# Moving small vector steps to GpSimd and ScalarE, routing ahead of other steps, and a constant product in rounds without a step: attention with a sparse expert layer, one core

## The chip, the cores and the metric

The kernel runs on 1 core of one Trainium2 chip. The time is device microseconds (us) of that core for one execution, from three runs, of which the median is given. A separate execution was profiled; its trace gives the durations of single instructions. Engines are written as in the profile: PE is TensorE's matmul, PEld its weight load, DVE is VectorE, ACT is ScalarE, POOL is GpSimd, SP is SyncE.

## The reference

Input x has shape (8, 512, 128): 8 sequences (B) of T = 512 rows with D = 128. All is float32.

```python
q, k1, k2, v = heads(x @ Wq.T), heads(x @ Wk1.T), heads(x @ Wk2.T), heads(x @ Wv.T)   # 16 heads of 8
a1 = softmax(causal(q @ k1 / sqrt(8)));  a2 = softmax(causal(q @ k2 / sqrt(8)))
attn = a1 - sigmoid(lambda)[head] * a2
attn = attn / max(sum(abs(attn)), 1e-6)
x = layernorm(x + (attn @ v) @ Wo.T)
xn = layernorm(x) * gamma + beta                     # the expert layer, 8 experts, 2 per row
probs = softmax(xn @ router_w.T / 1.5);  w, idx = top_k(probs, 2)
y = sum over the 2 experts of w * (silu(xn @ W1[e]) @ W2[e])        # W1: 128x512, W2: 512x128
out = layernorm(x + y)
```

## The kernel before, in words

**Attention by units.** A unit (class `Unit`) is one sequence b and one group j of 32 queries for all 16 heads; its keys reach L = 32(j+1). Four heads share the 128 partitions, so a unit has four groups g of four heads. There are 8 x 16 = 128 units. Up to L = 256 a unit is called early and has 2 slots of scores (both softmaxes of two groups in one tile); above that it has 4 slots (two groups, one softmax). This makes 8 x (8 x 2 + 8 x 4) = 384 rounds, one per slot.

**What a slot goes through.** `scores` (PE, L327 and the causal mask L336, tile `sc`, two buffers), `maxima` (DVE, L349 and L357, negated row maxima `nm`), `exps` (ACT, L367, tile `et`, with the row sums in `sums`). After a unit's last slot, `combine` runs by pieces (two groups at a time for early units, one group for others): `ratios` (L379, L382, L383: three small DVE instructions that make c2, the ratio of the two softmax sums times lambda, once a unit), then per group a DVE scalar_tensor_tensor (L393, tile `junk`, only its row sum is kept: it gives the sum of absolute values), then per group a POOL multiplication of the second softmax by -c2 in place (L403), and where L isn't a multiple of 128 a POOL copy `rest` (L417). Then `transposes` (PE, L448, one tile `pt` with one buffer, first and second softmax accumulated in PSUM), `evacuate` (ACT, L473, tile `aT`) and `times_v` (PE, L490, tile `po`).

**A round** (`round_of`, L1107) issues one stage of each on the engines' in-order queues, which are written out by hand here: `times_v` of the unit that is through, `scores` of the slot ahead, `evacuate`, the list `on_act`, `maxima` of the present slot, `transposes`, the list `on_dve`, `combine` of the piece or pieces that are due, `exps` of the present slot, the list `on_dve_late`. Then it hands out other steps, which put PE work at the round's end and push what reads its result on one of the lists, for the next round.

**The other steps.** Five steps for each block of 128 rows (`block_tasks`: normalise, project out and residual, norms, turn, logits) and five for the next sequence's projections (`projection_tasks`: x turned, q, k1, k2, v) share one deque, `misc`, one step a round. When a chunk of blocks (6, 9, 9, 6 and 2 blocks) is complete, `route_tasks` go through `routing`, one a round beside `misc`: top-2 choice, counts by PE, places of the rows. Then `moves` send the rows to their places in memory by indirect DMA on POOL (L777), one a round. `experts` are the steps of `sparse_tasks` for tiles of 128 rows: `turn` (PE turns the rows, L871, tile `pa`; DVE scales them by gamma and beta, L874, tile `xgT`; the second matmul of an earlier tile goes in the same PSUM tile, L880, and ACT copies it out and stores it, L890) and `hidden` (first matmul L900, tile `pz`; tanh on ACT L845; product on DVE L847, tile `hT`). The last chunk of two blocks takes `dense_tasks`. A step takes one unit of `room`, of which a round has 2; `due` and `pace` spread the experts' steps, with arrival times that `times` estimates. `gathers` fetch the results by indirect DMA on POOL (L925), mix them (L935), normalise and store (L826).

**PSUM.** Eight banks: `ps_s` two tiles `sc` of two banks, `ps_t` one, `ps_o` one, `ps_m` two tiles `pm` for all the other steps, `pa` and `pz` among them.

**After the attention** some 40 rounds without a slot take two experts' steps each; this tail holds most of the last sparse chunk (19 tiles) and the dense chunk.

Of the kernel before, what the change touches and what calls it, by code (L numbers as in the profile page):

```python
# [20 lines left out]
def kernel(  # L21
# [43 lines left out]
    nhalf = const.tile([P, CB], F32, name="nhalf")  # L65
    rank = const.tile([P, CB, E], F32, name="rank")
# [45 lines left out]
    with ExitStack() as actx:  # L112
# [123 lines left out]
        def projection_tasks(b):  # L236
# [10 lines left out]
            def transpose_x():  # L247
                pm = ps_m.tile([P, NT, P], F32, tag="pm", name=f"pmx_{b}")
                for c in range(NT):
                    nc.tensor.transpose(pm[:, c, :], xts[b][:, c, :], ident)  # L250
                on_dve.append(lambda: nc.vector.tensor_copy(xT, pm))

            def project_q():
# [13 lines left out]
                def spread():  # L267
                    nc.vector.tensor_copy(qs, pm)
                    on_pool.extend(lambda h=h: spread_head(h) for h in range(4))

                on_dve.append(spread)
# [6 lines left out]
            def project_v():  # L278
# [4 lines left out]
                def keep():  # L283
                    nc.vector.tensor_copy(vt, pm)
# [5 lines left out]
                on_dve.append(keep)  # L290
# [3 lines left out]
        class Unit:  # L294
# [80 lines left out]
            def ratios(self):  # L375

                sums, jj = self.blk["sums"], self.jj
                c1 = sp.tile([P, NG], F32, tag="c1", name=f"c1_{self.b}_{self.j}")
                nc.vector.tensor_mul(c1, sums[:, 0, jj, :], slam)  # L379
# [3 lines left out]
                nc.vector.tensor_mul(self.c2, c1, r2)  # L383

            def combine(self, piece):
# [5 lines left out]
                L = self.L  # L391
                for g in piece:
                    nc.vector.scalar_tensor_tensor(  # L393
                        junk[:, :L],
                        self.et[:, g, 1, :L],
                        self.c2[:, g : g + 1],
                        self.et[:, g, 0, :L],
                        ALU.mult,
                        ALU.max,
                        accum_out=self.blk["big"][:, self.jj, g : g + 1],  # L400
                    )
                for g in piece:
# [7 lines left out]
                    )  # L410
                for gs, lo, kw in self.blocks(piece):
# [86 lines left out]
        def block_tasks(b, i, blk):  # L498
# [88 lines left out]
            def turn():  # L587
# [4 lines left out]
                else:  # L592
                    s["xnT"] = ch.xnT[:, ci, :]
                on_dve.append(
                    lambda: nc.vector.tensor_scalar(s["xnT"], pm, gam, bet, ALU.mult, ALU.add)
# [9 lines left out]
        def route_tasks(ch):  # L605
# [57 lines left out]
            def weights():  # L663
                def step():
# [6 lines left out]
                    if ch.sparse:  # L671
# [5 lines left out]
                        ch.w = [r["rc"], cp.tile([P, CB], F32, tag="w2nd", name=f"w2nd_{n0}")[:, :nb]]  # L677
                        ch.w[0] = cp.tile([P, CB], F32, tag="w1st", name=f"w1st_{n0}")[:, :nb]
# [61 lines left out]
            def rows():  # L740
                def step():
# [9 lines left out]
                    ch.row = cp.tile([P, 2, CB], U32, tag="row", name=f"row_{n0}")  # L751
# [43 lines left out]
            def together(*steps):  # L795
                def both():
                    for step in steps:
                        step()

                return both  # L800

            if not ch.sparse:
                return [largest, first, second, weights, go]
            tasks = [largest, first, second, together(weights, chosen), counts]
            tasks += [together(starts, rows), owners]
# [44 lines left out]
        def sparse_tasks(ch):  # L850
# [15 lines left out]
            def turn(t):  # L866
# [3 lines left out]
                if t < nt:  # L870
                    nc.tensor.transpose(pm[:, 0, :], xg[t], ident)  # L871
                    xgT[t] = gp_.tile([P, P], F32, tag="xgT", name=f"xgT_{n0}_{t}")
                    on_dve.append(
                        lambda: nc.vector.tensor_scalar(  # L874
                            xgT[t], pm[:, 0, :], gam, bet, ALU.mult, ALU.add
# [21 lines left out]
            def hidden(t):  # L897
                pz = ps_m.tile([P, NF, P], F32, tag="pm", name=f"pz_{n0}_{t}")
# [146 lines left out]
        misc, routing, experts, moves, gathers = (deque() for _ in range(5))  # L1045
# [18 lines left out]
        def times():  # L1064
# [8 lines left out]
            for ch in chunks:  # L1073

                behind = seq * (24 + (2 * ch.nb + 3 if ch.sparse else 0)) / 48
# [7 lines left out]
        def round_of(now=None, ahead=None):  # L1083
# [19 lines left out]
            run(on_dve)  # L1103
            left = now["left"] if now else 2
            for _ in range(-(-len(to_combine) // left)):
                v, piece = to_combine.popleft()
                v.combine(piece)  # L1107
                to_transpose.append((v, piece))
            if now:
# [5 lines left out]
            if misc:  # L1115
                misc.popleft()()
                room -= 1
            if routing:
                step = routing.popleft()
                step()  # L1120
                room -= step.__name__ == "counts"

# [18 lines left out]
            due = min(due, 4.0)  # L1141

        with tc.manual_schedule(
# [10 lines left out]
            run(on_dve)  # L1154
# [126 lines left out]
```

## Time and profile before

| | before |
|---|---|
| median of 3 runs | 1220.2 us (1216.8 to 1223.7) |
| the profiled execution | 1212.0 us, its span 1210.1 us |
| mean granted TensorE clock | 0.927 of full speed |
| first and last maxima of the attention | 19.0 us and 1084.9 us of the span |
| DVE busy, ACT busy, POOL busy | 927.1, 780.4, 526.8 us |
| DVE instructions that change: L379, L382, L383 | 175, 170, 178 ns, 128 of each |
| L874 `xgT`, L595 `xnT`, copies L251, L268, L284 | 407, 402, about 690 ns; 88, 32 and 24 of them |

A group of instructions is given as its line, engine, operation, output and inputs with partitions x elements, how many there are (x), then the busy time in us and the mean ns of one, and after a second bar how long the engine had been idle just before them and what ended that. A stretch ("windows") gives each engine's busy time in us with its number of instructions, the granted PE clock as a share of full speed, and the share of the DMA engines in use. A wait gives the engine and line that waited, what ended the wait, the total in us, how often, and the longest. A matmul of float32 is two instructions in the trace.

### The profile page before, as it was taken

The numbers are of one execution on the slowest core, as the hardware profiler recorded it, in microseconds if no ns is written. First come the engines' busy times: TensorE is split into PE (matmuls) and PEld (weight loads), VectorE is DVE, ScalarE is ACT, GpSimd is POOL, SyncE is SP. The second block draws the span as 40 slices with busy tenths as digits, with TensorE's granted clock in tenths as the row PEclk, the third lists the DMA queues.
The fourth block names the chain that finished last, engine by engine and source line by source line (L and its number), as shares of the span: only waits on it lengthen the run. The fifth ranks groups of instructions, "written<-read, shape, count | busy, mean of one in ns | idle before, by whom it ended". The sixth has DMA issues, their size and how long they took to land.

```text
span 1210.1 us, 28192 instructions
## 1 busy us (share of the span) xinstructions
PE 1093.9 (90%) x9450; PEld 776.2 (64%) x9450; DVE 927.1 (77%) x2837; ACT 780.4 (64%) x2775; POOL 526.8 (44%) x935
## 2 busy tenths in 40 slices
PE   5999899989999899989998999988999989997686
PEld 3566565555666566666666666666667667777675
DVE  4688778777887887987887878887767898874556
ACT  3678767576777777766766867774567566662221
POOL 4343433463423442267464432333554652444333
PEclk7699969797999999989998999997899799998998
DMA  4400000110221112100322222221213344444762
GB/s 133 122 8 1 10 2 8 31 56 30 50 63 46 54 32 67 45 27 27 93 69 58 73 54 68 64 73 31 81 52 91 95 120 124 122 123 129 207 177 67
DMA packets 128895, 84.28 MB, mean 70 GB/s; under 512 B 22896, under 2 KB 114288, under 8 KB 128752
## 3 DMA queue, kind: packets, MB, share of 16 engines
q1 hardware_dynamic: 111952, 68.26, 20.2%
q0 software_dynamic: 3840, 7.87, 2.3%
q10 hardware_dynamic: 12960, 6.36, 1.8%
q8 instruction: 75, 1.23, 0.4%
q14 instruction: 68, 0.56, 0.2%
HBM read 63.31 MB, written 17.56 MB: 67 GB/s over the span
## 4 chain that ended last, share of the span: by engine, by line
PE 60%; DVE 16%; ACT 11%; issue 6%; POOL 4%; DMA 3%; ACTq 1%; POOLq 0%; SPq 0%; DVEq 0%
PE pt L448 19%; PE sc L327 13%; ACT et L367 7%; PE po L490 5%; PE pz L900 5%; PE pa L880 5%; PE sc_None L327 5%; DVE junk L393 2%; DVE nm L357 2%; PE pmo L541 2%; ACT aT L473 2%; DVE nm L349 2%; POOL et L403 1%; DVE hT L847 1%; POOL xs L777 1%
## 5 line engine op out<-in xcount | busy, mean ns | idle before, releaser
L403 POOL TENSOR_SCALAR et<-et,c 128x224 f32<-128x224 f32 (+15 forms) x512 | 270.9, 534 | 458.1 <-DVE junk L393 295.0
L448 PE MATMUL pt<-ident,et 128*128 128x128 f32 (+1 forms) x2048 | 326.7, 296 | 26.8 <-ACT aT L473 14.9
L448 PEld LDWEIGHTS pt<-ident,et 128*128 128x128 f32 (+1 forms) x2048 | 230.5, 145 | 159.6 <-issue 58.2
L367 ACT ACTIVATE et<-sc,nm 128x512 f32<-128x512 f32 (+7 forms) x512 | 300.4, 595 | 48.7 <-DVE nm L357 27.6
L357 DVE TENSOR_REDUCE nm<-sc 128x2 f32<-128x576 f32 (+7 forms) x256 | 252.0, 984 | 45.1 <-PE sc L336 44.6
L473 ACT COPY aT<-pt 128x384 f32<-128x384 f32 (+5 forms) x488 | 186.1, 407 | 134.5 <-PE pt L448 130.7
L393 DVE SCALAR_TENSOR_TENSOR junk<-et,c 128x224 f32<-128x224 f32 (+15 forms) x512 | 258.6, 505 | 9.6
L327 PE MATMUL sc<-kT,qb 32*128 32x384 f32 (+7 forms) x1024 | 246.8, 559 | 10.9 <-ACT et L367 9.6
L367 ACT ACTIVATE et<-sc_None,nm 128x256 f32<-128x256 f32 (+7 forms) x512 | 188.6, 387 | 32.0 <-DVE nm L349 22.0
L327 PE MATMUL sc_None<-kT,qb 32*128 32x512 f32 (+7 forms) x512 | 116.5, 535 | 21.8 <-ACT et L367 21.0
L900 PE MATMUL pz<-xgT,w 128*128 128x128 f32 x704 | 102.1, 291 | 18.8 <-DVE xgT L874 18.5
L349 DVE TENSOR_REDUCE nm<-sc_None 128x4 f32<-128x256 f32 (+7 forms) x128 | 96.1, 751 | 29.6 <-PE sc_None L336 29.3
L327 PEld LDWEIGHTS sc<-kT,qb 32*128 32x128 f32 x1024 | 78.3, 187 | 61.3 <-ACT et L367 27.4
L367 ACT ACTIVATION_READ_ACCUMULATOR et<-sc_None,nm 128x1 f32 x512 | 108.1, 211 | 0.0
L900 PEld LDWEIGHTS pz<-xgT,w 128*128 128x128 f32 x704 | 92.5, 204 | 23.6 <-DVE xgT L874 21.2
L367 ACT ACTIVATION_READ_ACCUMULATOR et<-sc,nm 128x1 f32 x512 | 103.9, 203 | 0.0
L880 PE MATMUL pa<-w,hT 128*128 128x128 f32 x704 | 98.1, 285 | 0.6 <-ACT ysb L890 0.6
L845 ACT ACTIVATE th<-pz 128x512 f32<-128x512 f32 x88 | 52.7, 599 | 68.9 <-PE pz L900 47.9
L880 PEld LDWEIGHTS pa<-w,hT 128*128 128x128 f32 x704 | 90.9, 202 | 1.3 <-ACT ysb L890 0.7
L777 POOL DMA_INDIRECT xs<-xh,row x60 | 65.9, 1099 | 46.9 <-DMA xs<-xh,row 31.3
L490 PE MATMUL po<-aT,vt 128*32 128x128 f32 (+1 forms) x2048 | 85.3, 290 | 0.0
L847 DVE SCALAR_TENSOR_TENSOR hT<-th,pz 128x512 f32<-128x512 f32 x88 | 60.2, 684 | 30.8 <-ACT th L845 30.6
(150 smaller groups left out, 1281.0 us busy)
## 6 DMA issues: line engine op xcount, KB each, us to landing
w<-in_w_dram SPq DMA_DIRECT2D x192, 256.0 KB
xg<-xs SPq DMA_DIRECT2D x88, 64.0 KB
ys<-ysb ACTq DMA_DIRECT2D x88, 64.0 KB
xs<-zero SPq DMA_DIRECT2D x2, 1600.0 KB
xs<-zero SPq DMA_DIRECT2D x2, 1216.0 KB
xt<-in_x_dram SPq DMA_DIRECT2D x8, 256.0 KB
out_dram<-ot SPq DMA_DIRECT2D x32, 64.0 KB
vr<-vt SPq DMA_DIRECT2D x32, 32.0 KB
```

What stands on the lines that cost most here:

```text
L327: nc.tensor.matmul(parts[gi][:, :, :L], lhsT=qb[r, j].rearrange("p h q -> p (h q)"), rhs=kT[r, sets, :L], start=True, stop=False,)
L349: nc.vector.tensor_reduce(self.nm[:, g, :], sc.rearrange("p g (s l) -> p g s l", s=2)[:, :, :, : self.L], AX.X, ALU.max, negate=True,)
L357: nc.vector.tensor_reduce(self.nm[:, g, s], sc[:, :, : self.L], AX.X, ALU.max, negate=True)
L367: nc.scalar.activation(self.et[:, g, si, : self.L], sc[:, gi, lo : lo + self.L], AF.Exp, bias=self.nm[:, g, si : si + 1], accum_out=self.b ...
L393: nc.vector.scalar_tensor_tensor(junk[:, :L], self.et[:, g, 1, :L], self.c2[:, g : g + 1], self.et[:, g, 0, :L], ALU.mult, ALU.max, accum_ ...
L403: nc.gpsimd.tensor_scalar(self.et[:, g, 1, :L], self.et[:, g, 1, :L], self.c2[:, g : g + 1], -1.0, ALU.mult, ALU.mult,)
L448: nc.tensor.matmul(pt[: len(gs) * kw, x_, :], lhsT=lhsT, rhs=ident, is_transpose=True, start=(k == 0), stop=(k == 1),)
L473: nc.scalar.copy(self.aT[: rows[done], self.used + done : self.used + end, :], pt[: rows[done], done:end, :],)
L490: nc.tensor.matmul(self.blk["po"][32 * g : 32 * g + 32, self.jj, :], lhsT=v[:rows, kb, 32 * g : 32 * g + 32], rhs=self.aT[:rows, self.at[g ...
L777: nc.gpsimd.indirect_dma_start(ch.xs[:, :], bass.IndirectOffsetOnAxis(ap=ch.row[:, k, c : c + 1], axis=0), ch.xh[:, c, :], None,)
L880: nc.tensor.matmul(pm[:, 1, :], lhsT=hT[y][:, f, :], rhs=w[y][1][:, f, :], start=(f == 0), stop=(f == NF - 1),)
L900: nc.tensor.matmul(pz[:, f, :], lhsT=w[t][0][:, f * P : (f + 1) * P], rhs=xgT[t], start=True, stop=True,)
```

## The change

- The projections' copies out of PSUM (`xT`, `qs`, `vt`), and the scaling by gamma and beta of the turned rows (`xnT` of a block, `xgT` of an expert's tile), go from DVE to ACT; the latter as an activation (Identity) with a scale and a bias per partition. The DMAs on SP that follow `vt` stay.
- `ratios`: a new step `weighted`, issued at the end of the round of a unit's last slot, makes c1 on POOL; for units above L = 256 also c2, by a power of -1 and a product on POOL. Early units keep the reciprocal and one product on DVE.
- `combine` for L <= 96: POOL's multiplication comes first, and the sum of absolute values is taken late in the round from the product, for two groups by one scalar_tensor_tensor and one reduction.
- In a round `on_dve` runs after `combine`, not before it.
- Routing goes first: in a round with a routing step no step of `misc` is taken. Projections have their own deque, after `misc`. Two pairs of routing steps are taken apart, so a sparse chunk's routing is 10 steps and not 8.
- `keep_busy`: in a round of the attention in which no step took room, PE multiplies a bf16 tile of ones (128x128) by 512 columns of ones into a tile `pm` that nobody reads.
- After the attention the experts' first matmul writes to `ps_s` tiles. Row places and weights of a chunk have 3 buffers instead of 2; one number in `times` goes from 24 to 22.

```diff
-                on_dve.append(lambda: nc.vector.tensor_copy(xT, pm))
+                on_act.append(lambda: nc.scalar.copy(xT, pm))
...
-                    nc.vector.tensor_copy(qs, pm)
+                    nc.scalar.copy(qs, pm)
...
-                    nc.vector.tensor_copy(vt, pm)
+                    nc.scalar.copy(vt, pm)
...
-                nc.vector.tensor_mul(c1, sums[:, 0, jj, :], slam)
+                if self.c2 is not None:
+                    return
...
-                nc.vector.tensor_mul(self.c2, c1, r2)
+                nc.vector.tensor_mul(self.c2, self.c1, r2)
+
+            def weighted(self):
+                self.c1 = sp.tile([P, NG], F32, tag="c1", name=f"c1_{self.b}_{self.j}")
+                nc.gpsimd.tensor_tensor(self.c1, self.blk["sums"][:, 0, self.jj, :], slam, ALU.mult)
+                if not self.early:
+                    self.c2 = sp.tile([P, NG], F32, tag="c2", name=f"c2_{self.b}_{self.j}")
+                    nc.gpsimd.tensor_tensor(
+                        self.c2, self.blk["sums"][:, 1, self.jj, :], mone, ALU.pow
+                    )
+                    nc.gpsimd.tensor_tensor(self.c2, self.c1, self.c2, ALU.mult)
...
+                    if small:
+                        both = junk[:, : m * L].rearrange("p (g l) -> p g l", g=m)
+                        nc.vector.scalar_tensor_tensor(both, second, -1.0, first, ALU.mult, ALU.max)
+                        nc.vector.tensor_reduce(big[:, g0 : g0 + m], both, AX.X, ALU.add)
+                        return
...
+                if small:
+                    on_dve_late.append(largest)
...
-                    lambda: nc.vector.tensor_scalar(s["xnT"], pm, gam, bet, ALU.mult, ALU.add)
+                    lambda: nc.scalar.activation(
+                        s["xnT"], pm, AF.Identity, bias=bet, scale=gam
+                    )
...
-            tasks = [largest, first, second, together(weights, chosen), counts]
-            tasks += [together(starts, rows), owners]
+            tasks = [largest, first, second, weights, chosen, counts]
+            tasks += [starts, rows, owners]
...
-                        lambda: nc.vector.tensor_scalar(
-                            xgT[t], pm[:, 0, :], gam, bet, ALU.mult, ALU.add
+                        lambda: nc.scalar.activation(
+                            xgT[t], pm[:, 0, :], AF.Identity, bias=bet, scale=gam
...
-                pz = ps_m.tile([P, NF, P], F32, tag="pm", name=f"pz_{n0}_{t}")
+                pool, tag = (ps_s, "sc") if attention_done else (ps_m, "pm")
+                pz = pool.tile([P, NF, P], F32, tag=tag, name=f"pz_{n0}_{t}")
...
+        def keep_busy():
+            pm = ps_m.tile([P, T], F32, tag="pm", name="pmw")
+            nc.tensor.matmul(
+                pm, lhsT=ones, rhs=ones.unsqueeze(1).to_broadcast([P, 4, P]), start=True, stop=True
+            )
...
-            run(on_dve)
             left = now["left"] if now else 2
             for _ in range(-(-len(to_combine) // left)):
                 v, piece = to_combine.popleft()
                 v.combine(piece)
                 to_transpose.append((v, piece))
+            run(on_dve)
...
-            if misc:
-                misc.popleft()()
-                room -= 1
             if routing:
                 step = routing.popleft()
                 step()
                 room -= step.__name__ == "counts"
+            elif misc or proj:
+                (misc or proj).popleft()()
+                room -= 1
+            if now and now["left"] == 1:
+                now["u"].weighted()
...
+            if now and room == 2:
+                keep_busy()
```

## The prediction

> **What bounds the kernel now.** I read the page first: shares, the row of granted clocks, the chain that ended last.
>
> ```profile
> span 1210.1 us, 28192 instructions
> ...
> PE 1093.9 (90%) x9450; PEld 776.2 (64%) x9450; DVE 927.1 (77%) x2837; ACT 780.4 (64%) x2775; POOL 526.8 (44%) x935
> ...
> PEclk7699969797999999989998999997899799998998
> ...
> PE 60%; DVE 16%; ACT 11%; issue 6%; POOL 4%; DMA 3%; ACTq 1%; POOLq 0%; SPq 0%; DVEq 0%
> ```
>
> PE carries 60% of the chain; DVE, which the change relieves, 16%. The clock falls below full speed in some twenty of forty slices. Next, stretches of the trace, in pairs at the same place of a sequence (by the maxima, one a round): units 4 to 7 cold (151) and warm (410), unit 13 cold (221) and warm (353), rounds without another step (85), a warm sequence's early units (386), the tail's sparse part (1089).
>
> ```profile
> 151.20:173.10 21.90, 21.90 (x118) 12.85 (x116) 14.33 (x53) 13.26 (x57) 7.87 (x18) 0.57 0.00 1
> 410.20:427.10 16.90, 14.87 (x129) 9.88 (x130) 14.82 (x55) 14.04 (x59) 7.97 (x18) 1.00 0.15 40
> 221.10:241.10 20.00, 19.92 (x105) 12.41 (x105) 11.99 (x34) 10.12 (x31) 11.25 (x14) 0.57 0.15 46
> 353.30:367.40 14.10, 13.70 (x121) 9.66 (x119) 12.21 (x36) 10.46 (x31) 4.76 (x8) 1.00 0.19 52
> 85.50:105.60 20.10, 19.98 (x187) 12.17 (x190) 17.27 (x43) 17.54 (x57) 6.76 (x12) 1.00 0.01 1
> 386.40:429.90 43.50, 37.63 (x377) 26.85 (x379) 35.20 (x135) 33.69 (x154) 19.42 (x41) 1.00 0.18 53
> 1089.00:1166.00 77.00, 55.15 (x439) 50.24 (x440) 42.23 (x134) 20.21 (x47) 27.78 (x33) 0.91 0.60 168
> ```
>
> Order: length, then PE, PEld, DVE, ACT, POOL, clock, DMA. The cold stretches take 21.9 for 16.9 us and 20.0 for 14.1, with fewer matmuls: 23% and 30% of cold time is lost. In long rounds (85) PE is full by its modelled ends, with ACT (17.5 of 20.1) and DVE (17.3) close behind: three engines in balance. In early units (386) PE has 5.9 us free of 43.5, DVE 8.3.
>
> **DVE relief.** Removed, by these rows and the same list's 402 ns for L595 and about 690 for the three copies:
>
> ```profile
> L874 DVE TENSOR_SCALAR xgT<-pa,gam,bet 128x128 f32<-128x128 f32 x88 | 35.8, 407 | 56.7 <-ACT ysb L890 45.8 <-PE pa L871 6.6 <-issue 2.8
> L383 DVE TENSOR_TENSOR c<-c,r 128x4 f32<-128x4 f32 x128 | 22.7, 178 | 7.0 <-DVE r L382 0.9
> L379 DVE TENSOR_TENSOR c<-sums,slam 128x4 f32<-128x4 f32 x128 | 22.4, 175 | 2.4 <-ACT et L367 2.4
> L563 POOL TENSOR_TENSOR l_rs<-l_ve,nhalf 128x2 f32<-128x2 f32 x32 | 23.2, 725 | 47.3 <-DVE c L379 33.5 <-DVE l_ve L559 13.7
> L90 POOL TENSOR_TENSOR l_rs<-l_ve,nhalf 128x1 f32<-128x1 f32 x32 | 19.0, 593 | 30.8 <-DVE l_ve L88 28.4 <-DVE c L379 2.1
> ```
>
> 64 x (175 + 170 + 178) = 33.5; 64 x 175 = 11.2; 24 x 0.69 = 16.5; 32 x 0.402 = 12.9; 88 x 0.407 = 35.8: 110 us. Besides, DVE stands 45.8 us before `xgT` until ACT has copied the same PSUM tile. In long rounds none of it counts, as PE is full. In early units about 11 (c1) + 6 (half of `xnT`) + 9 (a third of the tiles before the tail) + 13 (a third of 40 us of that standing) = 39 us leave DVE; PE's free time there, 5.9 x 8 = 47, allows it. I take 14, a third, since a round's DVE work is often covered by ACT or PE: ends 0 and 39. For L <= 96 two groups' sums cost much the same either way (at L = 64 two times 285 + 83 ns before; after, one instruction of 128 elements at 354 and a reduction at 286): 0, ends -2 and +2.
>
> **ACT load.** 24 copies of 512 at 0.59 (ACT's `kT` row) are 14 us. `xnT` and `xgT`: ACT's plain 128x128 copy is 268 ns, its exponential of 128x128 with one bias operand 369; a second operand makes 0.46, and 120 of them 55 us. They go ahead of `exps` on ACT, and behind `exps` wait the next scores, which share two PSUM tiles. PE's weight loads wait for `exps` on 109 occasions in 384 rounds (28%). Of about 119 such additions outside the tail, 28% at 0.47 are 15; two thirds lie in rounds where the same step gives PE about 1 us: +5, ends 0 and +55 (all on the path).
>
> **Ratios on POOL.** No row shows a POOL power over four columns. 593 ns for one and 725 for two give 0.99 for four; two products near POOL's shortest multiplication (128x32, 294 ns) make 1.6 us from the last exponential to c2, against DVE's 0.52. Here a rule speaks against the change: the Trainium skill (GPSIMD Engine Reference, Engine selection) wants elementwise work on VectorE, GpSimd being about twice slower with two inputs. By the rule c2 would be about 0.5 us later; by the row 1.1. The row decides. On POOL the `moves`, `gathers` and the next multiplication queue behind this wait for `exps`; on DVE `junk` and what follows. But today `junk` starts 1.5 us after a long unit's last exponential (median of 64; quartiles 0.8 and 2.2), behind `on_dve` and the ratios, which now go behind or away. With each unit's own slack of the transposes behind it (median 0.8 us), a c2 1.7 us late adds 10 us of PE standing and earlier starts give 9 back. About a third of the rounds also carry an indirect DMA on POOL, so some 20 of 64 units find it occupied: +5, ends -9 and +25.
>
> **The constant product.** Counting the steps that the planner's deques hand out round by round, 111 of 384 rounds take none now, and 113 after: 113 products. No row shows a bf16 product of 512 columns; a float32 pass of 512 (L275) takes about 0.5 us in a pair, so 0.2 to 0.5. I take 0.25, as bf16 needs fewer passes: 28 us. PE is without an instruction for 0.27 us on average in such a round when warm, mostly before the next scores: +6, ends 0 and +50.
>
> **The clock.** (1 - 0.927) x 2 x 1210.1 = 177 us at half clock: about 37 at the start, 27 in the tail, 113 between. How it falls:
>
> ```profile
> 216.00:218.00 2.00, 1.46 (x19) 0.56 (x11) 1.90 (x8) 0.07 (x1) 0.35 (x1) 1.00 0.02 4
> 218.00:220.00 2.00, 0.97 (x7) 0.73 (x9) 1.93 (x7) 1.54 (x5) 0.38 (x2) 1.00 0.00 0
> 220.00:222.00 2.00, 1.93 (x12) 0.95 (x10) 2.00 (x4) 1.44 (x6) 1.81 (x2) 0.80 0.46 122
> 222.00:224.00 2.00, 2.00 (x7) 0.83 (x8) 1.36 (x7) 1.69 (x5) 0.86 (x2) 0.50 0.58 177
> ```
>
> PE was idle in pieces of about 1 us, none near 3. The Trainium skill (TensorE: Matmul & The Clock Gate, Why this matters for your kernels) asks for no idle gap over about 3 us between bursts; by that rule the fall wouldn't come, and filling such pieces would gain 0. By the rows the clock falls on low activity: adding up the columns that PE streams between the clock's changes (3.41 us apart), nearly all falls follow a span with the fewest. One product a round would lift most of those. Of the falls before the tail, about half are in rounds that get a product (routing at 219 and 512, first units at 650); others (549, 627, 955) are not. Half of 113 at 26% is 15; the first twelve rounds, all with a product, may warm some 15 us sooner: 4. Sum -19, ends 0 and -33.
>
> **The tail.** The sparse part runs 25 rounds in 77 us, 3.1 each, though PE needs 2.2: `pz` waits for the tile that `xgT` and `ysb` release, and for `xgT` behind DVE's queue. With `ps_s` and `xgT` on ACT both waits go. Next late: POOL's two fetches, 1.0 each, with a 0.59 power, in 11 rounds; and weights, at DMA share 0.60 for 3.1 us, so about 1.9 a round at full share. I take 0.4 x 11 + 0.4 x 12 = 9 less one round more by my count (3): -6, ends +2 and -15.
>
> **Order and routing.** `on_dve` behind `junk` delays block steps by 0.6 us in 160 rounds, most within a round's slack, while `junk` itself comes earlier; two more routing rounds a chunk and blocks held back 8 rounds move work, not add it; the SP queue gets the 8 `vt` DMAs from ACT instead, with expert loads behind them. Third buffers: no wait names these tiles, 0. Together +1, ends -5 and +10.
>
> **Sum.** -14 + 5 + 5 + 6 - 19 - 6 + 1 = -22, against the profiled execution's own 1212.0 (span 1210.1 and 1.9 around it). The median lies 8.2 higher; I put the difference on it: 1198.
>
> **Rivals.**
> - The gate doesn't answer to one product (0.15): clock term 0, 1198 + 19 = 1217, no change. For it: the idle pieces are partly POOL's and DMA's, as at 549. Against: the sums of columns.
> - ACT becomes the bound (0.23), slower: at 85 ACT is busy 17.5 of 20.1, and its additions come ahead of `exps`. From the point where a round's ACT work passes PE's, each addition counts in full and DVE's relief is worth nothing. With half of them there: 30 instead of 5, and the 14 lost: 1198 + 25 + 14 = 1237; with all of them 1262. Against: rounds with an expert's step give PE more than ACT.
> - The likeliest (0.62) has its own range, 1168 to 1213.
> - A change that doesn't do what it says: products placed where PE is full (long rounds hold 65 of 113). Then +28 for +6: 1220; within the second case's chance.
>
> **Range and chances.** About 0.5% (1214 to 1226) is what a measurement can tell from no change. Faster 0.62, same 0.15, slower 0.23. Range 1165 to 1240: the first case's bounds and most of the third.
>
> **What would show it.** Right: mean clock above 0.95, no cold stretch in the routing rounds, early sequences below 43.5 us, the tail's sparse part near 70 us, DVE near 820 us, POOL near 640. Wrong: clock unchanged with 113 products; PE's waits for `exps` grown well over 114 us; PE or DVE waiting for POOL's c2; the rounds of 85 to 105 longer than 2.0 us each.

## The result and the profile after

The changed kernel takes 1267.1 us (median of 6 runs, 1252.0 to 1279.3) beside 1218.8 us of the kernel before in the same series: a ratio of 1.034, 95% interval 1.026 to 1.041. It is slower by 3.4%; 1198 us had been forecast, and the time lies above the range. The profiled execution spans 1250.3 us. Ratios in this document compare the runs within 1.5% of the fastest of the same kernel, which of e2, e7 and e12 below are only three of six and so lean to the fast side; the mean of all runs is given beside them and is the safer figure there, because most of the spread goes with the granted clock.

The page of the changed kernel, in the same rows as before:

```profile
span 1250.3 us, 28180 instructions
...
PE 1119.4 (90%) x9564; PEld 783.2 (63%) x9564; DVE 859.7 (69%) x2341; ACT 829.7 (66%) x2919; POOL 637.4 (51%) x1192
...
PEclk7579969999999999988989899997899998998999
...
PE 52%; DVE 14%; ACT 11%; POOL 9%; issue 8%; DMA 4%; ACTq 1%; POOLq 0%; DVEq 0%
```

DVE is relieved by 67 us (860 where the prediction looked for 820), and POOL is at 637 (640 foretold). But PE has gone from 60% to 52% of the chain, POOL from 4% to 9% and "issue" from 6% to 8%: the end is now set less by work on PE and more by what PE waits for. The mean clock of this execution, 0.928, is that of before (0.927), 114 products notwithstanding. Cut by unit (from one maxima to the next), the attention's units above L = 256 are 42.8 us longer in the two profiled executions, the early units 6.5 longer, and the tail 7.3 shorter.

The groups that the change made, after the second bar the idle time before them and what ended it:

```profile
L416 DVE SCALAR_TENSOR_TENSOR junk<-et,c 128x128 f32<-128x128 f32 (+12 forms) x416 | 238.1, 572 | 93.6 <-POOL c L395 86.2 <-ACT et L369 1.8
...
L392 POOL TENSOR_TENSOR c<-sums,mone 128x4 f32<-128x4 f32 x64 | 65.5, 1024 | 51.6 <-ACT et L369 51.0
...
L1073 PE MATMUL pmw<-ones 128*128 128x512 bf16 x114 | 48.8, 428 | 1.9 <-POOL ones L1232 1.9
...
L897 ACT ACTIVATE xgT<-pa,bet,gam 128x128 f32<-128x128 f32 x88 | 40.5, 461 | 48.0 <-PE pa L903 42.1 <-issue 5.7
...
L389 POOL TENSOR_TENSOR c<-sums,slam 128x4 f32<-128x4 f32 x128 | 25.5, 199 | 85.6 <-ACT et L369 85.2
...
L395 POOL TENSOR_TENSOR c<-c,c 128x4 f32<-128x4 f32 x64 | 12.7, 199 | 5.0
```

Two single prices were foreseen: 1024 ns for the power (0.99 us estimated), 461 ns for the scaled activation (0.46). The constant product takes 428 ns where 250 were taken. What was not foreseen in this size: 93.6 us of DVE's idle time stand just before `junk`, and 86.2 of them end with POOL's c2. The kernel before had 9.6:

```profile
L393 DVE SCALAR_TENSOR_TENSOR junk<-et,c 128x224 f32<-128x224 f32 (+15 forms) x512 | 258.6, 505 | 9.6
```

The waits say the same (total in us, how often, longest), and show the next link:

```profile
DVE nm L359 <- PE sc L338: 97.1, 99, 3.6
DVE junk L416 <- POOL c L395: 86.2, 63, 3.6
POOL c L389 <- ACT et L369: 85.2, 46, 7.9
...
POOL c L392 <- ACT et L369: 51.0, 37, 3.5
...
PEld pmr L554 <- POOL rexp L549: 15.4, 14, 1.7
```

The matching waits of before:

```profile
DVE nm L357 <- PE sc L336: 44.6, 61, 3.1
...
PEld pmr L526 <- POOL rexp L521: 4.5, 4, 1.7
```

DVE waits for c2 63 times in the 64 long units, 1.4 us each. POOL itself stands 136 us before its first product and its power, with other work queued behind; one such piece is `rexp`, for which PE then stands. DVE's wait for the scores `sc` has more than doubled: the whole pipeline runs later. In time, at the first long unit of the first sequence, among the next one's projections (start, length, engine, line, operation, tiles, idle time and its releaser):

```profile
71.09 1.03 POOL L392 TENSOR_TENSOR c<-sums,mone 128x4 f32<-128x4 f32 x1 [2.85 <-ACT et L369]
...
72.21 0.20 POOL L395 TENSOR_TENSOR c<-c,c 128x4 f32<-128x4 f32 x1
...
72.38 0.69 POOL L260 TENSOR_SCALAR qb<-qs,hms 128x512 f32<-128x512 f32 x1
72.44 0.93 DVE L416 SCALAR_TENSOR_TENSOR junk<-et,c 128x288 f32<-128x288 f32 x1 [1.39 <-POOL c L395]
...
73.01 0.83 POOL L549 COPY rexp<-rd 128x512 f32<-128x512 f32 x1
...
73.89 1.01 PE L554 MATMUL pmr<-ident,rexp 128*128 128x128 f32 x4 [1.34 <-POOL rexp L549]
```

POOL has stood for 2.85 us, holding `qb` and `rexp` behind the wait; then power, product, `qb` and `rexp` go one after the other, and DVE stands 1.39 us and PE 1.34. The first product, c1, isn't in this chain: it ran at 68.05, as the first softmax's sums come a slot earlier.

### The profile page after: what moved, and what is told of

It is laid out like the page before. It is cut to its first block, busy times and chain, and to the rows that moved or that the text cites. A ratio compares the mean times of both kernels' runs of the same rounds, so it can differ in the third digit from the quotient of the medians.

```text
span 1250.3 us, 28180 instructions
## 1 busy us (share of the span) xinstructions
PE 1119.4 (90%) x9564; PEld 783.2 (63%) x9564; DVE 859.7 (69%) x2341; ACT 829.7 (66%) x2919; POOL 637.4 (51%) x1192
## 4 chain that ended last, share of the span: by engine, by line
PE 52%; DVE 14%; ACT 11%; POOL 9%; issue 8%; DMA 4%; ACTq 1%; POOLq 0%; DVEq 0%
PE pt L476 16%; PE sc L329 11%; ACT et L369 8%; PE po L518 5%; PE sc_None L329 5%; PE pa L903 4%; PE pz L925 4%; DMA xs<-xh,row 3%; DVE junk L416 3%; POOL c L392 2%; POOL et L429 2%; PE pmo L569 2%; DVE nm L359 2%; ACT aT L501 2%; DVE nm L351 1%
## 5 line engine op out<-in xcount | busy, mean ns | idle before, releaser
L429 POOL TENSOR_SCALAR et<-et,c 128x224 f32<-128x224 f32 (+15 forms) x512 | 275.2, 544 | 316.7 <-DVE junk L416 265.2
L476 PE MATMUL pt<-ident,et 128*128 128x128 f32 (+1 forms) x2048 | 322.3, 294 | 27.3 <-ACT aT L501 16.8
L416 DVE SCALAR_TENSOR_TENSOR junk<-et,c 128x128 f32<-128x128 f32 (+12 forms) x416 | 238.1, 572 | 93.6 <-POOL c L395 86.2
L329 PE MATMUL sc<-kT,qb 32*128 32x384 f32 (+7 forms) x1024 | 249.5, 564 | 17.6 <-ACT et L369 16.5
L329 PE MATMUL sc_None<-kT,qb 32*128 32x512 f32 (+7 forms) x512 | 112.6, 522 | 22.9 <-ACT et L369 22.3
L392 POOL TENSOR_TENSOR c<-sums,mone 128x4 f32<-128x4 f32 x64 | 65.5, 1024 | 51.6 <-ACT et L369 51.0
L903 PEld LDWEIGHTS pa<-w,hT 128*128 128x128 f32 x704 | 88.2, 197 | 1.6 <-issue 0.9
L807 POOL DMA_INDIRECT xs<-xh,row x60 | 69.5, 1158 | 36.6 <-DMA xs<-xh,row 29.2
```

Of the source, the lines that this page charges most:

```text
L329: nc.tensor.matmul(parts[gi][:, :, :L], lhsT=qb[r, j].rearrange("p h q -> p (h q)"), rhs=kT[r, sets, :L], start=True, stop=False,)
L392: nc.gpsimd.tensor_tensor(self.c2, self.blk["sums"][:, 1, self.jj, :], mone, ALU.pow)
L416: nc.vector.scalar_tensor_tensor(junk[:, :L], second[:, k], self.c2[:, g : g + 1], first[:, k], ALU.mult, ALU.max, accum_out=big[:, g : g ...
L429: nc.gpsimd.tensor_scalar(self.et[:, g, 1, :L], self.et[:, g, 1, :L], self.c2[:, g : g + 1], -1.0, ALU.mult, ALU.mult,)
L476: nc.tensor.matmul(pt[: len(gs) * kw, x_, :], lhsT=lhsT, rhs=ident, is_transpose=True, start=(k == 0), stop=(k == 1),)
L903: nc.tensor.matmul(pm[:, 1, :], lhsT=hT[y][:, f, :], rhs=w[y][1][:, f, :], start=(f == 0), stop=(f == NF - 1),)
```

## The experiments

The theories on record: **A**, the ratios on POOL; as A1 because c2 comes late, as A2 because POOL's queue is held. **B**, the order of steps. **C**, ACT is full. **D**, the constant product costs PE more than the clock gives back. Every kernel is the changed kernel with the edit shown, and was timed beside the kernel before; differences between two experiments are differences of these ratios. The clock is the mean over all runs of a kernel (before: 0.920 to 0.924).

| | ratio to before, 95% interval | mean of all runs | clock |
|---|---|---|---|
| changed kernel | 1.034 (1.026 to 1.041) | 1.038 | 0.914 |
| e1 DVE's ratios | 0.998 (0.995 to 1.000) | 1.000 | 0.939 |
| e2 no product | 1.021 (1.012 to 1.031) | 1.031 | 0.914 |
| e3 old order | 1.017 (1.011 to 1.023) | 1.021 | 0.933 |
| e4 turned rows on DVE | 1.039 (1.033 to 1.044) | 1.039 | 0.917 |
| e5 e1, c1 on POOL | 0.996 (0.992 to 1.000) | 0.996 | 0.942 |
| e6 e1, POOL's chain unused | 1.011 (1.006 to 1.015) | 1.015 | 0.930 |
| e8 e1, no product | 0.995 (0.991 to 0.998) | 0.999 | 0.925 |
| e7 e8, old order | 0.977 (0.973 to 0.981) | 0.984 | 0.934 |
| e11 e8, projections as before | 0.984 (0.978 to 0.990) | 0.985 | 0.933 |
| e12 e7, c1 on POOL | 0.975 (0.969 to 0.981) | 0.984 | 0.938 |
| e9 e7, with product | 0.988 (0.982 to 0.993) | 0.991 | 0.941 |
| e10 e7, turned rows on DVE | 0.990 (0.987 to 0.992) | 0.991 | 0.935 |
| e16 e7, tail's tiles as before | 0.986 (0.979 to 0.992) | 0.988 | 0.934 |
| e15 e7, list ahead of combine | 1.000 (0.997 to 1.003) | 1.002 | 0.918 |
| e13 e1, product in routing rounds | 0.990 (0.987 to 0.993) | 0.995 | 0.930 |
| e14 e1, two products | 0.998 (0.995 to 1.001) | 1.001 | 0.950 |

**One part undone (e1 to e4).** For e1 all three steps of the ratios go back to DVE:

```diff
-                if self.c2 is not None:
-                    return
+                self.c1 = sp.tile([P, NG], F32, tag="c1", name=f"c1_{self.b}_{self.j}")
+                nc.vector.tensor_mul(self.c1, sums[:, 0, jj, :], slam)
...
-            if now and now["left"] == 1:
-                now["u"].weighted()
```

> The changed kernel with the three small ratio instructions back on VectorE (no GpSimd power or product). Theory A (the late ratio: GpSimd's power makes c2 over 1 us later, VectorE stands 86 us before the scalar_tensor_tensor and the whole round slips): 20 to 30 us less than the changed kernel's 1267, about 1240. Rival B (order of steps: block steps right behind their reciprocals wait for GpSimd's rexp): within 8 us of 1267. Rival C (ScalarE is full): within 5 us. Rival D (the constant product costs PE time): within 5 us.

3.6% comes back, some 44 us where theory A had asked for 20 to 30: the ratios alone account for the loss. e2 takes the product away:

```diff
-            if now and room == 2:
-                keep_busy()
```

> The changed kernel without the constant product. Theory A: within 5 us of 1267. Rival B: the same. Rival C: the same. Rival D (114 products of about 0.3 us each on PE, and no better clock): 15 to 30 us less, 1237 to 1252, mean clock unchanged. If the product does lift the clock, as predicted: slower than 1267 and a lower mean clock.

The product costs the changed kernel 1.2% (0.7% by the means) at an unchanged clock of 0.914. The two intervals overlap, so the cost itself isn't clear of noise; that the product brings this kernel no gain is. e3 restores the order:

```diff
-            if routing:
-                step = routing.popleft()
-                step()
-                room -= step.__name__ == "counts"
-            elif misc or proj:
-                (misc or proj).popleft()()
-                room -= 1
+            if misc:
+                misc.popleft()()
+                room -= 1
+            if routing:
+                step = routing.popleft()
+                step()
+                room -= step.__name__ == "counts"
...
-                        proj.extend(projection_tasks(b + 1))
+                        misc.extend(projection_tasks(b + 1))
```

> The changed kernel with the deques as before: one deque for block steps and projections, one step of it and one of routing a round. Theory A: within 8 us of 1267. Rival B: the projections again lie between a block's reciprocals and its normalise step in the second block, so PE no longer waits for rexp there: 20 to 30 us less, about 1242, the gain at units 9 and 10. Rivals C and D: within 5 us (fewer products would lower it by a few us under D).

1.7% comes back. e4 gives DVE the turned rows and the projections' copies again (the five `nc.scalar` operations of the change back to `nc.vector`, `on_act` to `on_dve`):

```diff
-                on_act.append(lambda: nc.scalar.copy(xT, pm))
+                on_dve.append(lambda: nc.vector.tensor_copy(xT, pm))
```

> The changed kernel with xT, qs, vt, xnT and xgT back on VectorE. Theory A and rivals B and D: 0 to 10 us slower than 1267, as VectorE gets 65 us of work back. Rival C (ScalarE is full, so its additions ahead of the exponentials count): 20 to 50 us less, 1217 to 1247.

Nothing comes back: theory C, my rival of ACT as the bound, falls for this kernel.

**Late, or in the way? (e5, e6).** e5 keeps c1 on POOL, now for all units, but takes the reciprocal and the last product to DVE:

```diff
-                if not self.early:
+                if False:
```

> The changed kernel with GpSimd's c1 kept for all units, still issued behind the exponentials, but the reciprocal and the product on VectorE for all units (no power). Theory A1 (the 1.0 us power makes c2 late): as with all ratios on VectorE, about 1213 to 1220. Rival A2 (GpSimd stands in its queue until the exponentials are through, and what lies behind it there is late): most of the loss stays, 1250 to 1267.

It is as fast as e1: one short product on POOL that waits for an exponential does no harm, and c1 on POOL, for early units too, has no part in the loss. e6 lets DVE make the c2 that is used, and leaves POOL's wait, product, power and second product standing, for a result that nobody reads (so it has work that the reference doesn't need):

```diff
+                nc.vector.tensor_mul(self.c2, sums[:, 0, jj, :], slam)
+                nc.vector.tensor_mul(self.c2, self.c2, r2)
...
-                    self.c2 = sp.tile([P, NG], F32, tag="c2", name=f"c2_{self.b}_{self.j}")
                     nc.gpsimd.tensor_tensor(
-                        self.c2, self.blk["sums"][:, 1, self.jj, :], mone, ALU.pow
+                        self.c1, self.blk["sums"][:, 1, self.jj, :], mone, ALU.pow
                     )
-                    nc.gpsimd.tensor_tensor(self.c2, self.c1, self.c2, ALU.mult)
+                    nc.gpsimd.tensor_tensor(self.c1, self.c1, self.c1, ALU.mult)
```

> The changed kernel with the ratios that are used made on VectorE, while GpSimd still waits for the exponentials and makes its two products and the power into a tile that nobody reads (added work, the result doesn't depend on it). Theory A1 (c2 late for VectorE): 1213 to 1222. Rival A2 (GpSimd's queue held by the wait and occupied for 1.4 us in 64 rounds): 1245 to 1267.

It came between the two expectations: 1.3% of the 3.6% is the held queue (A2), and by difference 2.3% the lateness (A1), which no run has alone. The waits tell them apart too. In e6:

```profile
POOL c L390 <- ACT et L369: 93.2, 45, 8.2
...
POOL c L392 <- ACT et L369: 54.5, 42, 3.6
...
PEld pmr L554 <- POOL rexp L549: 13.2, 12, 1.8
```

and in e5:

```profile
POOL c L389 <- ACT et L369: 90.7, 46, 7.1
...
PEld pmr L554 <- POOL rexp L549: 1.2, 3, 0.6
```

POOL's first wait, for c1, is equally long in both, 91 and 93 us, and costs nothing in e5. In e6 a second wait of 54.5 us follows, since the power needs the last exponential's sums, and then the power itself. Both stand ahead of `rexp`: it starts 1.22 us after its input on the mean of 32 in e5 and 1.83 in e6, and PE waits for it. In the stretch of the changed kernel above the input was ready at 69.12, 2.0 us before the second wait ended, and power, product and `qb` then took 1.9 more; which of them costs more no run separates.

**Parts together (e7 to e12).** e8 is e1 without the product, e7 besides with e3's old order, e11 with the projections alone back in `misc` (routing still first), e12 is e7 with e5's c1 on POOL, e9 is e7 with the product, e10 is e7 with e4's edit.

> The changed kernel with three parts undone at once: ratios on VectorE, no constant product, deques as before; what stays is ScalarE's copies and turned rows, on_dve behind combine, the small units' sums, and the tail's PSUM tiles. If the three losses add up (45 + 15 + 20 us by the single runs, against 1213 of before in that call): 1267 - 80 = 1187, that is 0.975 to 0.985 of before. If they overlap (all three are ways to lengthen the same rounds): 1205 to 1215, 0.995 to 1.0.

> The changed kernel with ratios on VectorE and no constant product. If the product costs about 15 us whatever stands beside it: 0.985 of before and the mean clock as before (0.927). If the product lifts the clock (0.944 with it and VectorE's ratios) and that pays for its PE time: 1.0 to 1.01 of before, and a mean clock of 0.93 or less.

> Ratios back on VectorE and the old order of steps (one deque for blocks and projections, a step of it and a routing step in one round); the constant product stays, now in fewer rounds, since with the old order fewer rounds are left without a step at other places. Theory D (the product costs PE about what the clock gives back, as it did under the new order with VectorE's ratios, where it was worth -0.2% to +0.5%): 0.975 to 0.985 of the kernel before, the same as with all three parts undone (0.977), at a granted clock near 0.945. Rival: where the pipeline isn't stretched the product pays as the prediction had it (-13 us net, 1.1%): 0.960 to 0.970.

> Ratios on VectorE, no constant product, old order, and also the turned rows and the projections' copies back on VectorE: what is left of the change is the order of the two sums for the shortest units, VectorE's list behind combine, the tail's tiles, and the buffers. Theory A (the moves to ScalarE relieve VectorE as the prediction had it, -14 + 5 = -9 us): 0.98 to 0.99 of the kernel before. Theory C (ScalarE's load costs what VectorE's relief gives, or more): 0.970 to 0.979, no slower than with the moves (0.977). If these moves are worth all that the three-undone kernel gained: 1.00.

> Ratios on VectorE, no constant product; routing still goes first, but the projections are back in the blocks' deque, in order of arrival. It tells the two halves of the order apart: with both halves new 0.995 was measured, with both old 0.977. Theory B (the projections behind all blocks' steps let a block's normalise meet its reciprocals a round earlier, in rounds 20 to 27, so that PE waits for GpSimd's rexp): 0.977 to 0.983, most of the 1.8% comes back. Rival B2 (it is the routing that takes the rounds of the blocks, and late blocks hold back the rest): 0.990 to 0.997, nothing comes back.

> As the kernel with three parts undone (VectorE's ratios, no product, old order: 0.977), but c1 alone stays on GpSimd, for all units, with the reciprocal and one product on VectorE. Theory A (only a c2 from GpSimd is late; c1 has a whole row sum earlier to come, and relieves VectorE by 175 ns a unit): 0.970 to 0.977. Theory A2 (any GpSimd instruction that waits for the last exponential holds up its queue): 0.980 to 0.990.

With three parts undone the rest of the change is a gain: e7 takes 1198.0 us beside 1217.9, and e12 is the same within its interval. Both are faster than the kernel before and the changed kernel. (That 1198 is also the forecast is chance.) The old order is worth 1.8% (e8 to e7), and the projections bring 1.1% of it (e8 to e11; by the means 1.4 of 1.5%); with the product in place it is worth less, 1.0% (e1 to e9; 0.9% by the means). The product costs 1.1% (e7 to e9), the moves to ACT are worth 1.3% (e7 to e10), 0.7% each by the means, which with e7's six runs is at the edge of what can be told from nothing. c1 on POOL brings nothing either way. Of the expectations, e8 fell between its two, e9 came slower than both, and e11 just past the range of theory B.

What the projections' deque does is read from units 9 and 10 of the first sequence, at full clock in both. Stretch of e11, then of e8 (length, PE, PEld, DVE, ACT, POOL, clock, DMA):

```profile
65.90:83.70 17.80, 17.39 (x150) 10.84 (x149) 13.77 (x39) 14.28 (x46) 8.42 (x16) 1.00 0.08 13
```

```profile
65.90:83.70 17.80, 16.19 (x141) 10.22 (x143) 14.18 (x39) 13.22 (x44) 9.15 (x17) 1.00 0.01 2
```

PE is idle for 0.4 us with the old place of the projections and for 1.6 with the new. The steps in e11, in time:

```profile
66.87 1.13 PE L277 MATMUL pmk<-xT,wk_sb 128*128 128x512 f32 x2
...
69.26 1.12 PE L277 MATMUL pmk<-xT,wk_sb 128*128 128x512 f32 x2
...
72.04 1.06 PE L283 MATMUL pmv<-wv_sb,xT 128*128 128x128 f32 x8
...
74.28 0.60 PE L554 MATMUL pmr<-ident,rexp 128*128 128x128 f32 x4
```

and in e8:

```profile
65.74 1.13 PE L277 MATMUL pmk<-xT,wk_sb 128*128 128x512 f32 x2
...
68.12 0.66 PE L554 MATMUL pmr<-ident,rexp 128*128 128x128 f32 x4
...
69.66 0.81 PE L329 MATMUL sc<-kT,qb 32*128 32x320 f32 x4 [0.88 <-ACT et L369]
...
78.79 1.02 PE L277 MATMUL pmk<-xT,wk_sb 128*128 128x512 f32 x2
```

In e8 the block's steps come between the projections. Two of them are short on PE (0.3 us) and give DVE and ACT work of a whole block; PE waits for the exponentials meanwhile (0.88 us in one round). Units 9 and 10 take 9.4 and 8.7 us instead of 8.7 and 8.2: 1.2 us. In the five sequences that have these units at full clock in both traces the two are from 0.5 us shorter to 1.3 us longer, 0.6 longer on the mean, so about 4 us in the seven sequences that project for a next one. That this idle time also lowers the clock (0.925 for 0.933) would give most of the rest; that link is argued, by the runs below, and not tried alone.

**The clock (e13, e14).** In e13 the product is issued only in rounds that took a routing step, which left 19 products and not the 35 to 40 I expected; in e14 twice wherever the change has one.

```diff
-            room = 2
+            room, routed = 2, bool(routing)
...
-            if now and room == 2:
+            if now and room == 2 and routed:
```

> VectorE's ratios and the new order of steps, with the constant product only in those free rounds that carry a routing step, some 35 to 40 instead of 114. Base cases: 0.995 without any product, 0.998 with all. Theory D1 (the price lies in the long rounds that PE fills, the gain in the routing rounds, where the falls lay): clock near 0.935 to 0.94, time 0.980 to 0.989 of the kernel before. Theory D2 (the falls that matter aren't prevented by a product): clock 0.925 to 0.93, time 0.992 to 0.998.

> VectorE's ratios and the new order, two constant products in each free round instead of one (228 for 114, some 48 us more of PE work). Theory D1 (a product in a full round is on the path with all its 0.42 us): about 65 of the 114 second ones lie in long rounds, and half or more of their 27 us comes out as time, less a little more clock: 1.008 to 1.020, at a clock of 0.94 to 0.95. Rival (PE has room, and the first product was only too little for the gate): clock above 0.95, and 0.985 to 0.998.

e13 gained 0.5% (0.4% by the means) on e8, within the intervals of both, and less than D1 asked for; the clock rose by 0.005. With so few products it settles little. e14 came at e1's time, the upper end of the rival's range, at a clock between the two expectations: the rows of its clock and products are

```profile
PEclk8599999999999999989999799999899999998998
```

```profile
L1073 PE MATMUL pmw<-ones 128*128 128x512 bf16 x228 | 75.1, 408 | 4.0 <-POOL ones L1231 2.4 <-DVE hT L870 1.3
```

So with DVE's ratios the clock does answer: 0.925 without, 0.939 with 114, 0.950 with 228 products. (In the changed kernel it did not: 0.914 with and without.) What this is worth can be estimated from runs of one and the same kernel: in e1's 23 and e14's 22 runs time and clock go together (correlation -0.99 and -0.98) at 10.7 and 9.5 us for each 0.01. (Over the other kernels it is 6.5 to 12, over the kernel before 4 to 8, where the clock varies less; that the time follows the clock, and not the clock the time, is taken here and not shown.) By 10 us each, the first 114 products should have brought 13 us in e1 (0.0132) and the next 114 12 us (0.0119). The means show no gain: e1 1214.7 beside e8's 1216.5 (whose kernel before ran 3.2 us slower), e14 no different from e1. So by this estimate 114 products cost some 13 to 15 us on the path, out of 48 us of their own. From e7 to e9 the same sum gives 8 us by the clock against a loss of 9: a price of 17.

**The rest of e7's gain (e15, e16).** e15 runs `on_dve` ahead of `combine` again, e16 gives the tail's first matmuls the tiles `pm`; both else as e7.

```diff
+            run(on_dve)
             left = now["left"] if now else 2
...
-            run(on_dve)
```

```diff
-                pool, tag = (ps_s, "sc") if attention_done else (ps_m, "pm")
-                pz = pool.tile(
+                pz = ps_m.tile(
```

> The kernel with ratios, product and order undone (0.977 of the kernel before; 0.984 by the mean of all its runs), with VectorE's list run ahead of combine again. Theory L1 (the list behind combine lets the sum of absolute values, and with it GpSimd's product and PE's transposes, start earlier, which is worth more than the list's longer instructions): slower, 0.983 to 0.990. Rival L2 (the list's instructions beside GpSimd's product, 0.2 us longer each, cost as much as the earlier start gives): 0.972 to 0.980.

> The same kernel with the experts' first matmul after the attention back in the two tiles that all other steps share. As the prediction had it (the tail's tiles are worth 6 us): 0.982 to 0.986, and a tail some 6 us longer than 116.6. Rival (the tail waits for transfers and for ScalarE's tanh, and its tiles don't matter): 0.975 to 0.979.

e16 came in the direction of the prediction: 0.9% (0.4% by the means, not clear of noise), and a tail of 123.2 us instead of 116.6 in the profiled executions; the kernels that keep both of the tail's edits have 112.7 to 121.2. e15 missed both expectations, upward: the whole gain of e7 is gone, 2.3% (1.8% by the means), and the clock is 0.918 for 0.934. So without the list behind `combine` the other gains don't count: list, moves to ACT and tail, each undone alone from e7, cost 2.3, 1.3 and 0.9%, together twice what e7 gains. They don't add up. How the list's place brings its gain is open. In the profiled executions of e15 and e7, both at a clock of 0.92, the long units are not longer without it (680.2 and 688.7 us); the early ones are, 405.7 for 386.3 us, and 34 us more of them run at half clock.

## Why the prediction was wrong, point by point

The time from a long unit's last exponential to the start of `junk` (DVE) and of the first multiplication by c2 (POOL) decides when PE's transposes may start. Median and quartiles over 64 units of each profiled execution, in us:

| | `junk` starts | POOL's multiplication starts |
|---|---|---|
| before | 1.51 (0.77 to 2.23) | 2.72 (1.61 to 3.27) |
| changed | 1.41 (1.41 to 1.50) | 2.38 (2.24 to 2.96) |
| e6, POOL's chain unused | 0.69 (0.49 to 0.98) | 1.82 (1.43 to 2.85) |
| e7, DVE's ratios | 0.79 (0.50 to 1.07) | 1.67 (1.40 to 2.13) |
| e15, e7 with the list ahead | 0.85 (0.68 to 1.94) | 1.88 (1.42 to 3.33) |
| e10, e7 without the moves to ACT | 0.90 (0.64 to 1.18) | 1.85 (1.50 to 2.47) |

**Ratios on POOL: the step that failed, +5 with an upper end of 25.** It measured about 44 us (3.6% of 1219). The working priced c2 nearly rightly, 1.6 us after the last exponential estimated and 1.41 measured (the power and one product; the other product mostly ran before), and rightly saw that `junk` would otherwise come forward. But it set the one against the other and against the slack that the units of *before* had. The earlier start doesn't need POOL's ratios: with them on DVE, `junk` starts at 0.8 us, and either the moves to ACT (e15) or the list behind `combine` (e10) brings it near there. The right comparison was 0.8 against 1.4, in 63 of 64 units and not in some 20, each time with 0.6 to 0.7 us: 40 to 45 us if nothing covers it. By e6's split the lateness costs 2.3%, 28 us, so about a third is covered. What the list is worth (e15 to e7, 28 us by the ratios and 21 by the means) had been left inside that +5 as "earlier starts give 9 back". And the queue behind the power was named in the working and given no price of its own; e6 gives it 1.3%, 16 us. Two of the signs of being wrong on record came as written: a clock no higher with the products, and DVE waiting for POOL's c2. The wider rule that I let the row overrule, no elementwise work on GpSimd (the Trainium skill, GPSIMD Engine Reference, Engine selection), would have led to the better choice here, though not by its factor of two: c1, 199 ns on POOL and 175 on DVE, is free there (e5, e12). The cost is a power of 1024 ns (DVE's reciprocal takes 170) and a product behind it, between a unit's last exponential and all that follows.

**Order and routing: the second, +1 with an upper end of 10.** It measured 1.7 to 1.8%, 20 to 22 us (19 to 21 by the means), and 11 to 12 us where DVE made the ratios and the product stayed. "Move work, not add it" is true of the sums and false of the rounds: it didn't ask which round each moved step lands in, and whether that round has PE work to cover it. The waits of units 9 and 10 show this for the projections; how much of it is direct time and how much the lower clock stays open.

**Clock and product: the third, -19 and +6.** The mean clock was to pass 0.95; it stayed at 0.914 in the changed kernel and reached 0.939 where the ratios were back on DVE. By the estimate above the product's price was 13 to 17 us where +6 was taken, and its gain 8 to 13 where 19 was; in the changed kernel the gain was nothing (e2). One product takes 428 ns, not 250. My worry on record, products placed where PE is full, fits, as 65 of the 114 lie in long rounds, but no run has the products in early rounds alone. That the rounds stretched by POOL made idle time faster than one product could fill it is argued, not shown. The Trainium skill's rule of an idle gap of 3 us (TensorE: Matmul & The Clock Gate, Why this matters for your kernels) was no guide here: cold stretches come without such gaps, as the prediction argued; the count of columns in the last section tells them better.

**Right as a sum: DVE relief with ACT's load, -14 and +5.** -9 was predicted; e7 to e10 gives 1.3%, 16 us, or 8 by the means; the two parts were not measured apart. In the changed kernel the relief is invisible (e4), since DVE then stands waiting for c2 anyway. PE's waits for exponentials grew only from 114 to 129 us; the rival of ACT as the bound, 0.23 of the chances and the one that ended slower, had the sign and not the cause.

**Right: the tail, -6.** It became 7.3 us shorter. The wait that was to go is gone: PE's idle time before `pz`, 18.8 us and nearly all for DVE's `xgT`, before and after:

```profile
L900 PE MATMUL pz<-xgT,w 128*128 128x128 f32 x704 | 102.1, 291 | 18.8 <-DVE xgT L874 18.5
```

```profile
L925 PE MATMUL pz<-xgT,w 128*128 128x128 f32 x704 | 100.8, 289 | 0.0
```

The three terms that failed were set at -7 together (+5, +1, +6 and -19). Undone one at a time in the changed kernel they measured 44, 20 and 15 us, 79 in all; with 28 taken off for the list's gain that is 51, a miss of 58 us. The forecast lay 69 below the median. The parts don't add exactly, and the 15 isn't clear of noise, so this sum shows the size only. What no run separates is how much of each loss is a direct wait and how much the lower clock that goes with it: from e1 to the changed kernel the mean clock falls by 0.024, which at 10 us for 0.01 would be about half of the 45 us. The traces allow a second estimate. Take half of the time at half clock off the attention, and the changed kernel has 1034 us left and e1 1009: 25 us of direct waits.

## What to carry to other kernels

Compare a moved step with the best place that the same change makes possible, not with the present one: a gain that two edits bring together belongs to the one that brings it alone. A step between a late result and everything that needs it must be priced as a chain on its new engine, with what is queued behind it, even where that engine is half idle. And a reordering that adds no work still decides which rounds leave the bounding engine idle; read that round by round before calling it free.

## What was not expected of the hardware

VectorE's two-operand scaling (`x<-xa`) takes 348 ns in e15, where the list runs ahead of `combine` and none of the 30 overlaps GpSimd's multiplication, and 576 in e10, where 26 do:

```profile
L604 DVE TENSOR_SCALAR x<-xa,mv,l_rs 128x128 f32<-128x128 f32 x30 | 10.4, 348 | 0.0
```

```profile
L604 DVE TENSOR_SCALAR x<-xa,mv,l_rs 128x128 f32<-128x128 f32 x30 | 17.3, 576 | 0.0
```

The Trainium skill (SBUF — State Buffer, SBUF: two separate sides) has VectorE and GpSimd share a pair of ports that one instruction holds to its end, for some kinds of VectorE instructions; the 0.23 us agree in direction. It is 7 us of DVE in all, and far less than what the list's new place brings. POOL's power grows with its columns: 593 ns for one, 725 for two, 1024 for four, while its product of four columns takes 199, less than the shortest that the trace of before showed (294 for 128x32). Time and clock go together closely: about 10 us for each 0.01 of the mean, in e1's and e14's runs.

And the clock can be foretold from the matmuls. In the traces it is either full or half, and changes only at steps of 3.41 us. Count, in each such span, the columns that every matmul streams, times the share of the array's 128 rows and of its 128 columns that it uses, so that a score matmul on 32 rows counts a quarter. Over the 18 traces of this case, 275 of the 299 spans at full clock with fewer than 1500 such columns were followed by half clock, and 34 of the 5155 with more. PE was busy in up to 81% of such a low span, in more than 56% of half of them, so a busy PE of narrow matmuls does not by itself hold the clock; one constant product adds 512 to the span that it is in.
